# The delta rule of a two-layer model: four engines issue in the order written, steps end at each change of engine, the output gate runs ahead of the state's update, and score products move beside the state products

## Chip, cores and metric

The kernel runs on one NeuronCore of a Trainium2 chip. The core has TensorE (PE, matrix products), VectorE (DVE), ScalarE (ACT) and GpSimd (POOL), each with its own queue of instructions, and a SyncE queue (SP) that issues DMAs. TensorE writes its products to eight PSUM banks. The metric is the device time of one execution in microseconds, the median over several runs.

## What is computed

Two layers on 2 sequences of 1024 tokens, width 256, all float32. The first adds a gated delta rule and a mixture of low-rank experts to its input; the second adds gated linear attention and a sparse feed-forward. The change touches the delta rule alone:

```python
qkvz = hidden_states @ W_qkvz                      # 16 key heads, 32 value heads of 128
y = silu(causal_conv(concat(q, k, v), conv_w))     # 4 taps per channel
beta, g = sigmoid(b), -exp(A_log) * softplus(a + dt_bias)
q, k = l2norm(q) * DK**-0.5, l2norm(k)             # each shared by two value heads
def step(S, inp):                                  # one token, S is 128x128 per head
    S = S * exp(gt)
    kv = einsum('hk,hkv->hv', kt, S)
    S = S + kt[:, :, None] * ((vt - kv) * bt)[:, None, :]
    return S, einsum('hk,hkv->hv', qt, S)
gated = core * silu(z)
gated = gated * rsqrt(mean(gated * gated) + EPS) * norm_w
out = gated @ W_out
```

## The kernel before

**Tiling.** The token-by-token rule is computed in chunks of 64 tokens; a tile of 128 partitions holds a chunk of each of the two sequences (`LO` and `HI`). Eight groups of 4 value heads (2 key heads) are worked through one after the other, each in 4 units of 4 chunks. Two neighbouring chunks make a *pair*; there are 64 pairs. The state `k.S` of a group stays in SBUF.

**Stages.** The loop at L886 runs once per pair, and in each step several pairs are under way at different stages:

- `conv_block` (L327): for four blocks per step, a projection `pj` on TensorE, two evictions on ACT (`raw`, `conv`), three taps on DVE (L363), a Silu on ACT. GpSimd carries the three edge tokens over (`raw`, `tails`).
- `gates_part` (L391): norms of q and k (`sq`, `ssr`, `ss`, `rsqrt_pool`), and the gate `z` of two chunks.
- `pair_scores` (L489) for pair p: DVE accumulates the decays `lb`, ACT takes their exponential, GpSimd multiplies by beta (L512), TensorE makes the products `kq` of keys with keys and queries (L520), and DVE multiplies both into `np` (L526). SP sends `np` through DRAM to get 8x8 blocks (`n8`), which `pair_lanes` inverts on DVE.
- `pair_inverse` (L610) for pair p-1: joins the 8x8 inverses to 64x64 ones: products `px` and `pyt` on TensorE, copies `xs` on ACT, add to `U` and transpose `L` on DVE, masks `natm` on GpSimd.
- `chunk_tokens` (L675): keys and values transposed (`pk`, `pv`), scaled into `ktok` (GpSimd) and `vtok` (ACT).
- `chunk_state` (L701) for the two chunks of pair p-2: `pks`, `pqs` read the state; DVE corrects `vtok` (L719); GpSimd decays the state in place (L724); ACT scales `qs` (L729); `pf` and its copy `f`; then `pS`, which updates the state, and `po`, the output. DVE adds `pS` to `k.S` (L754), then makes `qs + po` (L758) and multiplies by `z` (L760); ACT sums the squares (`gsq`, L765). In the first chunk of a group there is no state yet: L716 to L729 and L758 are left out, and ACT copies `pS` (L752).
- `chunk_output` (L769): GpSimd makes the reciprocal root (`ms`, `rms`) and scales `z` (L782), TensorE transposes it (`yT`, L786), ACT copies (`yTs`, L788), TensorE multiplies by `W_out` (`out`, L792), DVE adds to the residual.

**What sets the order.** Each stage is a generator that yields between pieces. `in_windows` (L817) takes the pieces of a step in the order of due times: each stage has a window of the step, spread over the count of its yields in an earlier step. That is only the order in which the program is written down. A scheduler then orders the instructions of each engine anew by readiness, with the written order as priority; two `issue_after` blocks (L507, L557) tie single DVE instructions behind a tap. An engine works through its queue in the order that comes out: an instruction that waits holds up those behind it. PSUM tiles all come from one pool of eight banks (`ps_tile`).

## Time and profile before

| | |
|---|---|
| median of 3 runs | 2951.18 us (2948.95 to 2951.32) |
| profiled execution | 2948.61 us, of which the span is 2946.9 |
| delta rule, from first to last step | about 336 to 2570 us |
| granted TensorE clock in the steady stretch | 0.98 of full speed |
| DMA in the steady stretch | 16% of the 16 engines' time |

The profile comes from one execution. A busy time counts only working instructions; the rest of an engine's time is idle, and a list of waits tells which instruction's end ended each idle stretch. Matrix products overlap, so neighbouring ones show spans that lap over each other by about 0.1 us; the distance from start to start is what a product costs. Over all engines, the longest waits in 600 to 2400 us are (engine, line, waited for: total us, times, longest):

```profile
DVE vtok L719 <- PE pks L716: 202.7, 86, 4.2
ACT gsq L765 <- DVE z L760: 196.7, 81, 4.5
POOL raw L347 <- DVE conv L363: 148.2, 31, 6.2
```

These engines are idle for a third or more of the stretch, so such waits cost nothing by themselves.

### The profile page before, as it was taken

How to read it: one execution, taken by the hardware profiler on the slowest of the kernel's cores; microseconds unless marked ns; L12 is line 12 of the kernel's file. 1: busy time of each engine (PE TensorE's matmuls, PEld its weight loads, DVE VectorE, ACT ScalarE, POOL GpSimd, SP SyncE). 2: the span in 40 equal slices, each digit the busy share in tenths (PEclk: the TensorE clock that was granted, in tenths of full speed). 3: DMA queues.
4: the chain of work that ended last, by engine and by line, in shares of the span. 5: the costliest groups of instructions: out<-in, count | busy, mean ns of one | idle time of the engine just before them, and what ended most of it. 6: DMA issues, size and time to landing. Idle time of an engine off the chain costs nothing.

```text
span 2946.9 us, 87779 instructions
## 1 busy us (share of the span) xinstructions
PE 2647.8 (90%) x36502; PEld 1680.6 (57%) x36502; DVE 1914.8 (65%) x3845; ACT 1716.6 (58%) x4121; POOL 1516.5 (51%) x2690
## 2 busy tenths in 40 slices
PE   6998689998999899989999999999989998989997
PEld 2444356665666566655655666566655665654565
DVE  7652666676677666767767666677676677645544
ACT  4432566675666666666666667666666666544321
POOL 2222456666666666666666666666665666630000
PEclk9998899999999999999999999999999999999999
DMA  3001111111111111111111111111111111110000
GB/s 77 4 1 57 37 28 35 36 43 28 35 35 43 28 35 35 44 28 43 34 38 28 42 35 35 28 42 36 36 27 35 28 37 20 29 57 3 1 15 15
DMA packets 265965, 95.22 MB, mean 32 GB/s; under 512 B 220512, under 2 KB 244192, under 8 KB 265568
## 3 DMA queue, kind: packets, MB, share of 16 engines
q1 hardware_dynamic: 261872, 86.67, 13.2%
q8 instruction: 287, 4.70, 0.7%
q10 hardware_dynamic: 3696, 2.95, 0.4%
q14 instruction: 110, 0.90, 0.1%
HBM read 53.63 MB, written 27.53 MB: 28 GB/s over the span
## 4 chain that ended last, share of the span: by engine, by line
PE 32%; DVE 22%; ACT 13%; POOL 12%; issue 7%; DMA 7%; SPq 6%; DVEq 0%; POOLq 0%; ACTq 0%
DVE conv L363 6%; PE pj L152 5%; SPq L540 3%; PE out L792 3%; ACT gsq L765 3%; DMA n<-natd 3%; DVE qs L758 2%; DMA natd<-np 2%; DVE S L754 2%; POOL S L724 2%; DVE z L760 2%; PE y L1074 2%; POOL rn L447 2%; PE pg L152 2%; SPq L530 2%
## 5 line engine op out<-in xcount | busy, mean ns | idle before, releaser
L363 DVE SCALAR_TENSOR_TENSOR conv<-raw,convw,conv 128x512 f32<-128x512 f32 x768 | 644.3, 841 | 188.6 <-ACT conv L358 184.2
L152 PE MATMUL pj<-xnT,w 128*128 128x512 f32 x1024 | 509.4, 622 | 8.5 <-DMA w<-in_W_qkvz 8.5
L792 PE MATMUL out<-wo,yTs 128*128 128x256 f32 x1024 | 284.1, 425 | 106.7 <-ACT yTs L788 106.7
L719 DVE SCALAR_TENSOR_TENSOR vtok<-pks,neG,vtok 128x128 f32<-128x128 f32 x480 | 144.8, 342 | 251.7 <-PE pks L716 247.4
L765 ACT ACTIVATE gsq<-z 128x128 f32<-128x128 f32 x512 | 157.7, 308 | 246.3 <-DVE z L760 240.9
L152 PEld LDWEIGHTS pj<-xnT,w 128*128 128x128 f32 x1024 | 188.8, 197 | 187.0 <-issue 182.1
L792 PEld LDWEIGHTS out<-wo,yTs 128*128 128x128 f32 x1024 | 200.6, 206 | 143.0 <-ACT yTs L788 113.4
L724 POOL TENSOR_TENSOR S<-S,eEnd 128x512 f32<-128x512 f32 x224 | 257.7, 1170 | 26.7 <-PE pqs L716 26.3
L152 PE MATMUL z<-wz,xnT 128*128 128x512 f32 x512 | 240.4, 593 | 0.0
L356 ACT COPY raw<-pj 128x512 f32<-128x512 f32 x256 | 147.5, 576 | 144.3 <-PE pj L152 95.5
L754 DVE TENSOR_TENSOR S<-S,pS 128x512 f32<-128x512 f32 x224 | 148.5, 684 | 123.8 <-POOL S L724 110.8
L734 PE MATMUL pf<-vtok,invT 128*128 128x128 f32 x1024 | 167.1, 289 | 31.4 <-DVE vtok L719 31.2
L347 POOL COPY raw<-tails 128x6 f32<-128x6 f32 x192 | 68.8, 359 | 239.4 <-DVE conv L363 189.7
L358 ACT ACTIVATE conv<-pj,convw 128x512 f32<-128x512 f32 x256 | 176.9, 691 | 0.0
L729 ACT ACTIVATE qs<-pqs,neG 128x128 f32<-128x128 f32 x480 | 136.3, 365 | 56.9 <-PE pqs L716 54.9
L372 ACT ACTIVATE kq<-conv 128x512 f32<-128x512 f32 x128 | 81.3, 635 | 144.3 <-DVE conv L363 141.4
L734 PEld LDWEIGHTS pf<-vtok,invT 128*128 128x128 f32 x1024 | 135.9, 190 | 50.8 <-DVE vtok L719 43.2
L782 POOL TENSOR_TENSOR z<-z,rms 128x512 f32<-128x512 f32 x128 | 145.5, 1136 | 10.1 <-POOL rms L779 0.2
L688 POOL TENSOR_TENSOR ktok<-kt,wend 128x512 f32<-128x512 f32 x120 | 145.6, 1213 | 7.5 <-ACT kt L684 7.5
L360 POOL COPY tails<-raw 128x6 f32<-128x6 f32 x192 | 60.7, 316 | 156.5 <-ACT raw L356 156.5
L743 PE MATMUL pS<-f,ktok 64*64 64x128 f32 x3840 | 132.5, 275 | 7.6 <-ACT f L736 7.5
L603 PE MATMUL px<-L,natm 32*32 32x32 f32 x8192 | 101.7, 198 | 40.8 <-DVE L L645 22.7
(323 smaller groups left out, 5885.0 us busy)
## 6 DMA issues: line engine op xcount, KB each, us to landing
lb<-grows SPq DMA_DIRECT2D x128, 128.0 KB
natd<-np SPq DMA_DIRECT2D x128, 128.0 KB
w<-in_W_qkvz SPq DMA_DIRECT2D x16, 512.0 KB
nat<-np SPq DMA_DIRECT2D x256, 32.0 KB
n<-natd SPq DMA_DIRECT2D x512, 4.0 KB
ed<-E SPq DMA_DIRECT2D x64, 128.0 KB
U<-ed SPq DMA_DIRECT2D x64, 128.0 KB
wz<-in_W_qkvz SPq DMA_DIRECT2D x16, 256.0 KB
```

The source lines that it names most:

```text
L152: k.nc.tensor.matmul(ps, lhsT_of(kt), rhs_of(kt), start=(kt == 0), stop=(kt == KT - 1))
L356: nc.scalar.copy(chunks(raw[:, :, KSIZE - 1 :]), pv)
L358: nc.scalar.activation(chunks(y), pv, AF.Copy, scale=tap(KSIZE - 1))
L363: k.anchor = nc.vector.scalar_tensor_tensor(y, shifted, tap(j), y, ALU.mult, ALU.add).ins
L688: nc.gpsimd.tensor_tensor(pair(x.k), bcast(kt, 2, 2), bcast(wend, 3, P), ALU.mult)
L719: nc.vector.scalar_tensor_tensor(x.v[:, i, :], pks[:, i, :], at(k.neG, i), x.v[:, i, :], ALU.mult, ALU.add)
L724: nc.gpsimd.tensor_tensor(k.S[:, b], k.S[:, b], bcast(k.eEnd[:, b, t, h.h0 : h.h0 + HPG], 2, P), ALU.mult)
L734: nc.tensor.matmul(pf[:, i, :], invT[:, i, :], x.v[:, i, :], start=True, stop=True)
L754: nc.vector.tensor_tensor(k.S[:, b], k.S[:, b], pS[b], ALU.add)
L765: nc.scalar.activation(sq, x.z[:, i, :], AF.Square, accum_out=x.sumsq[:, i : i + 1])
L782: nc.gpsimd.tensor_tensor(y, y, bcast(rms, 2, P), ALU.mult)
L792: nc.tensor.matmul(po[:, 0:D], yT[:, i, :], wo[:, i, :], start=(i == 0), stop=(i == HPG - 1))
```

## The change

From `prefetch` to `pair_decays` the whole loop runs under `manual_schedule` for TensorE, ACT, DVE and GpSimd: these four take their instructions in the order in which the program is written down. SP's queue stays with the scheduler. The `issue_after` blocks go. Many more yields are set, one wherever the engine changes, so that `in_windows` interleaves the stages more finely. In `chunk_state` the lines for `qs + po` and `z` move ahead of the add to `k.S`, and the sums of squares move to the head of `chunk_output`. The products `kq` leave `pair_scores`: they become `pair_products`, called at the start of the state stage of the first chunk of pair p-2 in the same step (for the first two pairs, ahead of the step). The arithmetic is the same.

```diff
@@ conv_block, chunk_gate, unit_sums
     nc.scalar.activation(chunks(y), pv, AF.Copy, scale=tap(KSIZE - 1))
+    yield
...
-        k.anchor = nc.vector.scalar_tensor_tensor(y, shifted, tap(j), y, ALU.mult, ALU.add).ins
+        nc.vector.scalar_tensor_tensor(y, shifted, tap(j), y, ALU.mult, ALU.add)
         yield
@@ rsqrt_pool
     nc.gpsimd.tensor_tensor(out, x, k.mhalf[:, 0 : x.shape[1]], ALU.pow)
+    yield
     nc.gpsimd.tensor_tensor(t, out, out, ALU.mult)
...
     nc.gpsimd.tensor_tensor(out, out, t, ALU.mult)
+    yield
@@ pair_scores
-    with k.tc.issue_after(k.anchor):
-        nc.vector.tensor_tensor_scan(flat, flat, k.floor, -200.0, ALU.add, ALU.max)
+    nc.vector.tensor_tensor_scan(flat, flat, k.floor, -200.0, ALU.add, ALU.max)
     yield
     nc.scalar.activation(flat, flat, AF.Exp)
     yield
     nc.gpsimd.tensor_tensor(lb, lb, bcast(h.nb[:, c0 : c0 + PC], 3, CT), ALU.mult)
-    yield
-
-    kq = ps_tile(k, f"kq{pr.name}").rearrange("p (x m s i) -> p x m s i", x=PC, m=KPG, s=2)
-    for x in pr.chunks:
-        for m in range(KPG):
-            for b, rows in enumerate((LO, HI)):
-                both = of_chunk(h.kq[m], x.c, b)
-                nc.tensor.matmul(kq[rows, x.at, m], both[:, 0], both, start=True, stop=True)
     yield
     pr.np = pools.np.tile([P, 2, PC, HPG, CT], F32, tag="np", name=f"np{pr.name}")
     pairs = lambda a: a.rearrange("p x (m j) i -> p (x m) j i", m=KPG)
     for s in range(2):
-        by = kq[:, :, :, s].rearrange("p x m i -> p (x m) i")
+        by = pr.kq[:, :, :, s].rearrange("p x m i -> p (x m) i")
@@
+def pair_products(k, pr):
+
+    kq = ps_tile(k, f"kq{pr.name}").rearrange("p (x m s i) -> p x m s i", x=PC, m=KPG, s=2)
+    for x in pr.chunks:
+        for m in range(KPG):
+            for b, rows in enumerate((LO, HI)):
+                both = of_chunk(pr.h.kq[m], x.c, b)
+                k.nc.tensor.matmul(kq[rows, x.at, m], both[:, 0], both, start=True, stop=True)
+    pr.kq = kq
@@ pair_inverse, the same after each group of products
         blocks32(k, px, join, L)
         if s < 4:
             join = masked(s + 1)
+        yield
         xs = new("xs", s)
         nc.scalar.copy(xs, px)
@@ chunk_state
-def chunk_state(k, pools, x):
+def chunk_state(k, pools, x, scored=None):
...
+    if scored:
+        pair_products(k, scored)
     if not x.first:
         pks, pqs = four(k, f"pks{x.name}"), four(k, f"pqs{x.name}")
...
     yield
+    no = po
+    if not x.first:
+        nc.vector.tensor_tensor(qs, qs, po, ALU.add)
+        no = qs
+    nc.vector.tensor_tensor(x.z, no, x.z, ALU.mult)
+    yield
     if not x.last:
         for b in range(NB):
             if x.first:
...
                 nc.vector.tensor_tensor(k.S[:, b], k.S[:, b], pS[b], ALU.add)
     yield
-    no = po
-    if not x.first:
-        nc.vector.tensor_tensor(qs, qs, po, ALU.add)
-        no = qs
-    nc.vector.tensor_tensor(x.z, no, x.z, ALU.mult)
-    yield
+
+
+def chunk_output(k, pools, x):
...
     x.sumsq = pools.small.tile([P, HPG], F32, tag="sumsq", name=f"sumsq{x.name}")
@@ chunk_output
-    rsqrt_pool(k, sm, rms, ms, f"ch{x.name}")
+    yield
+    yield from rsqrt_pool(k, sm, rms, ms, f"ch{x.name}")
...
         nc.tensor.transpose(pt[:, i, :], y[:, i, :], k.ident)
+    yield
     yT = pools.work.tile([P, HPG, P], F32, tag="yT", name=f"yTs{x.name}")
     nc.scalar.copy(yT, pt)
@@ delta_layer
-        for p in range(-2, NPAIR + 3):
...
+        ordered = {nc.tensor.engine, nc.scalar.engine, nc.vector.engine, nc.gpsimd.engine}
+        with tc.manual_schedule(engines=ordered):
+            for p in range(-2, NPAIR + 3):
...
+                    if p < 2:
+                        pair_products(k, pair(p))
...
-                add("state0", 0.0, 0.5, chunk_state(k, pools, one))
+                    add("state0", 0.0, 0.5, chunk_state(k, pools, one, pair(p)))
```

More of the change, by code (lines that the diff above doesn't have):

```diff
@@ L398, in gates_part @@
         yield from unit_sums(k, pools, k.units[u + 1])
-        unit_norms(k, pools, k.units[u + 1])
-        yield
+        yield from unit_norms(k, pools, k.units[u + 1])
     if 0 <= p - 1 < NPAIR:
         for x in k.pairs[p - 1].chunks:
-            chunk_gate(k, pools, x)
-            yield
+            yield from chunk_gate(k, pools, x)
 def chunk_gate(k, pools, x):
@@ L461, in unit_norms @@
     r = sm.tile(shape, F32, tag="rn", name=f"rn{h.name}")
-    rsqrt_pool(k, sm, flat(r), flat(sse), f"un{h.name}")
+    yield
+    yield from rsqrt_pool(k, sm, flat(r), flat(sse), f"un{h.name}")
     h.norm = sm.tile([P, UCHUNK, KPG], F32, tag="norm", name=f"norm{h.name}", bufs=3)
@@ L469, in unit_norms @@
     nc.gpsimd.tensor_tensor(h.q2, h.rq, h.rq, ALU.mult)
+    yield
     rk2 = sm.tile([P, UCHUNK, KPG], F32, tag="rk2", name=f"rk2{h.name}")
@@ L482, in unit_norms @@
     nc.gpsimd.tensor_tensor(h.wend, h.nb, of(k.nrev), ALU.mult)
+    yield
 def four(k, name):
@@ L513, in pair_scores @@
     yield
-    kq = ps_tile(k, f"kq{pr.name}").rearrange("p (x m s i) -> p x m s i", x=PC, m=KPG, s=2)
-    for x in pr.chunks:
-        for m in range(KPG):
-            for b, rows in enumerate((LO, HI)):
-                both = of_chunk(h.kq[m], x.c, b)
-                nc.tensor.matmul(kq[rows, x.at, m], both[:, 0], both, start=True, stop=True)
-    yield
     pr.np = pools.np.tile([P, 2, PC, HPG, CT], F32, tag="np", name=f"np{pr.name}")
@@ L555, in at @@
         return bass.AP(a.tensor, flat(a)[:, r * W + c : r * W + c + 1].offset, [list(flat(a).ap[0])] + [[i * W + j, m] for i, j, m in dims])
-    with k.tc.issue_after(k.anchor):
-        nc.vector.tensor_copy(at(X, 0, 1, (2, 2, 4)), at(n, 0, 1, (2, 2, 4)))
+    nc.vector.tensor_copy(at(X, 0, 1, (2, 2, 4)), at(n, 0, 1, (2, 2, 4)))
     two, row, col = (4, 4, 2), (1, 0, 2), (0, 1, 2)
@@ L637, in pair_inverse @@
             join = masked(s + 1)
+        yield
         xs = new("xs", s)
@@ L642, in pair_inverse @@
         blocks32(k, pyt, xs, U)
+        yield
         nc.vector.tensor_tensor(U, U, pyt, ALU.add)
@@ L660, in pair_inverse @@
             nc.tensor.matmul(px[hi, i, :], full[lo, i, B:CT], L[lo, i, :], start=True, stop=True)
+    yield
     xs = new("xs", 5)
@@ L669, in pair_inverse @@
             nc.tensor.matmul(pyt[lo, i, :], xs[hi, i, :], U[hi, i, :], start=True, stop=True)
+    yield
     for q, copy in ((0, nc.scalar.copy), (2, nc.vector.tensor_copy)):
@@ L684, in chunk_tokens @@
         nc.scalar.copy(kt, pk[:, 0:KPG, :])
+        yield
         x.k = wk.tile([P, HPG, P], F32, tag="ktok", name=f"ktok{x.name}")
@@ L734, in chunk_state @@
         nc.tensor.matmul(pf[:, i, :], invT[:, i, :], x.v[:, i, :], start=True, stop=True)
+    yield
     f = wk.tile([P, HPG, P], F32, tag="f", name=f"f{x.name}")
@@ L748, in chunk_state @@
     yield
+    no = po
[3 more added lines that the diff above has]
+    nc.vector.tensor_tensor(x.z, no, x.z, ALU.mult)
+    yield
     if not x.last:
@@ L755, in chunk_state @@
     yield
-    no = po
-    if not x.first:
-        nc.vector.tensor_tensor(qs, qs, po, ALU.add)
-        no = qs
-    nc.vector.tensor_tensor(x.z, no, x.z, ALU.mult)
-    yield
+def chunk_output(k, pools, x):
+    nc, sm, wk, h, c = k.nc, pools.small, pools.work, x.h, x.c
     x.sumsq = pools.small.tile([P, HPG], F32, tag="sumsq", name=f"sumsq{x.name}")
@@ L766, in chunk_state @@
     yield
-def chunk_output(k, pools, x):
-    nc, sm, h, c = k.nc, pools.small, x.h, x.c
     wo = group_weights(k, pools, "o", h.grp)
@@ L777, in chunk_output @@
     rms = sm.tile([P, HPG], F32, tag="rms", name=f"rms{x.name}")
-    rsqrt_pool(k, sm, rms, ms, f"ch{x.name}")
+    yield
+    yield from rsqrt_pool(k, sm, rms, ms, f"ch{x.name}")
     nc.gpsimd.tensor_tensor(pair(rms), pair(rms), bcast(h.rq[:, c, :], 2, 2), ALU.mult)
@@ L786, in chunk_output @@
         nc.tensor.transpose(pt[:, i, :], y[:, i, :], k.ident)
+    yield
     yT = pools.work.tile([P, HPG, P], F32, tag="yT", name=f"yTs{x.name}")
@@ L792, in chunk_output @@
         nc.tensor.matmul(po[:, 0:D], yT[:, i, :], wo[:, i, :], start=(i == 0), stop=(i == HPG - 1))
+    yield
     res = k.res[:, h.t0 + c, :]
@@ L884, in delta_layer @@
         pair = lambda p: k.pairs[p] if 0 <= p < NPAIR else None
-        for p in range(-2, NPAIR + 3):
-            work = []
-            add = lambda kind, lo, hi, steps, *before: work.append((kind, lo, hi, steps, before))
-            prefetch(k, pools, p)
-            if p == NPAIR - 1:
-                silu_pending(k)
-            if p == -2:
-                for q in (0, 1):
-                    pair_decays(k, pools, pair(q))
-            add("conv0", 0.0, 0.475, conv_part(k, pools, p, 0))
-            add("conv1", 0.475, 0.95, conv_part(k, pools, p, 2), "conv0")
-            add(f"gates{p % 2}", 0.65, 1.0, gates_part(k, pools, p), "output1", "conv0")
-            if pair(p):
-                add("scores", 0.0, 0.45, pair_scores(k, pools, pair(p)))
-                add("lanes", 0.65, 0.9, pair_lanes(k, pools, pair(p)), "scores")
-            if pair(p - 1):
-                add("inverse", 0.0, 1.0, pair_inverse(k, pools, pair(p - 1)))
-                add("tokens0", 0.5, 1.0, chunk_tokens(k, pools, pair(p - 1).chunks[0]), "state0")
-            if pair(p - 2):
-                one, two = pair(p - 2).chunks
-                add("tokens1", 0.0, 0.4, chunk_tokens(k, pools, two))
-                add("state0", 0.0, 0.5, chunk_state(k, pools, one))
-                add("state1", 0.5, 1.0, chunk_state(k, pools, two), "state0", "tokens1")
-                add("output0", 0.55, 1.0, chunk_output(k, pools, one), "state0")
-            if pair(p - 3):
-                add("output1", 0.05, 0.5, chunk_output(k, pools, pair(p - 3).chunks[1]))
-            in_windows(k, *work)
-            if pair(p) and pair(p + 2):
-                pair_decays(k, pools, pair(p + 2))
@@ new lines, in delta_layer @@
+        ordered = {nc.tensor.engine, nc.scalar.engine, nc.vector.engine, nc.gpsimd.engine}
+        with tc.manual_schedule(engines=ordered):
+            for p in range(-2, NPAIR + 3):
+                work = []
+                add = lambda kind, lo, hi, steps, *before: work.append((kind, lo, hi, steps, before))
+                prefetch(k, pools, p)
+                if p == NPAIR - 1:
+                    silu_pending(k)
+                if p == -2:
+                    for q in (0, 1):
+                        pair_decays(k, pools, pair(q))
+                add("conv0", 0.0, 0.475, conv_part(k, pools, p, 0))
+                add("conv1", 0.475, 0.95, conv_part(k, pools, p, 2), "conv0")
+                add(f"gates{p % 2}", 0.65, 1.0, gates_part(k, pools, p), "output1", "conv0")
+                if pair(p):
+                    if p < 2:
+                        pair_products(k, pair(p))
+                    add("scores", 0.0, 0.45, pair_scores(k, pools, pair(p)))
+                    add("lanes", 0.65, 0.9, pair_lanes(k, pools, pair(p)), "scores")
+                if pair(p - 1):
+                    add("inverse", 0.0, 1.0, pair_inverse(k, pools, pair(p - 1)))
+                    add("tokens0", 0.5, 1.0, chunk_tokens(k, pools, pair(p - 1).chunks[0]), "state0")
+                if pair(p - 2):
+                    one, two = pair(p - 2).chunks
+                    add("tokens1", 0.0, 0.4, chunk_tokens(k, pools, two))
+                    add("state0", 0.0, 0.5, chunk_state(k, pools, one, pair(p)))
+                    add("state1", 0.5, 1.0, chunk_state(k, pools, two), "state0", "tokens1")
+                    add("output0", 0.55, 1.0, chunk_output(k, pools, one), "state0")
+                if pair(p - 3):
+                    add("output1", 0.05, 0.5, chunk_output(k, pools, pair(p - 3).chunks[1]))
+                in_windows(k, *work)
+                if pair(p) and pair(p + 2):
+                    pair_decays(k, pools, pair(p + 2))
```

## The prediction

> **What bounds the kernel now.** I read the page's busy table first, then the busy time of the delta rule's steady stretch (600 to 2400 us), then TensorE's waits in it, then one step on the timeline.

> ```profile
> span 2946.9 us, 87779 instructions
> PE 2647.8 (90%) x36502; PEld 1680.6 (57%) x36502; DVE 1914.8 (65%) x3845; ACT 1716.6 (58%) x4121; POOL 1516.5 (51%) x2690
> ```
> ```profile
> 600.00:2400.00 1800.00, 1649.40 (x26774) 1083.41 (x26774) 1243.29 (x2489) 1179.94 (x2938) 1133.32 (x2041) 0.98 0.16 35
> ```
> TensorE (first busy figure) works 1649.4 of 1800 us. The score products `kq` stand 50 times in this stretch, once per pair, so a step takes 36.0 us: 33.0 busy and **3.0 idle**. The change leaves TensorE's products as they are, so only those 3.0 us can be won: at most 62 steps x 3.0 = 186 us. What ends them:

> ```profile
> PE out L792 <- ACT yTs L788: 86.8, 44, 3.4
> PE pf L734 <- DVE vtok L719: 24.9, 38, 1.5
> PE pyt L669 <- DVE xs L663: 19.5, 13, 2.5
> PE px L603 <- DVE L L645: 10.6, 13, 1.1
> PE pS L743 <- ACT f L736: 5.6, 7, 1.0
> ```
> (Total us, times, longest.) More than half is one wait: the output product waits for ScalarE's copy `yTs`. No line names GpSimd: what it makes for TensorE, the scaled `z` that `yT` transposes, is early. The timeline of GpSimd in one step (start, us) shows why:

> ```profile
> 1259.52 1.04 POOL L782 TENSOR_TENSOR z<-z,rms 128x512 f32<-128x512 f32 x1
> 1260.52 1.56 POOL L512 TENSOR_TENSOR lb<-lb,nb 128x512 f32<-128x512 f32 x1
> ...
> 1263.64 2.48 POOL L724 TENSOR_TENSOR S<-S,eEnd 128x512 f32<-128x512 f32 x2
> ```
> `z` and `lb` go first, the decay of the state `S` last. That decay must wait for the products `pks` and `pqs`, which read the old state; in this step they end near 1261.2, and GpSimd is busy with the rest until 1263.6. DVE's add to `S` comes at 1268.94 and 1270.20, the next `pks` at 1275.56: 4.7 us of slack. So what is last today is the ACT copy, and GpSimd is off the path.

> **The change, part by part.** I compared the order of instructions in both programs, engine by engine.

> *Cheap parts.* ACT's table loads stay 154, so the exponential that moves into the first half of a step costs nothing in sum (1.28 us each). `kq` moves ahead of `pks` with the same 16 records (1.03 us): nothing gained, because its reader `np` waits for `lb` as well. No DMA is added; the loads of `lb` move by one place among SP's.

> *What goes.* ACT's copy `yTs` stood behind a projection's two evictions (`raw`, `conv`, 1.06 us from start to start) and up to three `gsq` (0.45 each); now the evictions come earlier and `gsq` after it. Of the 86.8/50 = 1.7 us per step nearly all goes. `pyt <- xs` and `px <- L` (0.6 per step) go too, as long as DVE isn't held.

> *What comes: GpSimd in issue order.* In the new order, after `pks` and `pqs` of a step's first chunk, GpSimd has: two `S`, one `natm`, two `ms`, `tails`, the power, `ktok`, four small ones, `lb`, the last `rms`, a small fill, and then `z`. The first waits for `pqs`, and everything is queued behind it. The rows:

> ```profile
> L724 POOL TENSOR_TENSOR S<-S,eEnd 128x512 f32<-128x512 f32 x170 | 195.8, 1171 | 20.2 <-PE pqs L716 20.2
> L782 POOL TENSOR_TENSOR z<-z,rms 128x512 f32<-128x512 f32 x100 | 114.3, 1143 | 7.8
> L688 POOL TENSOR_TENSOR ktok<-kt,wend 128x512 f32<-128x512 f32 x92 | 110.8, 1205 | 6.8 <-ACT kt L684 6.8
> L447 POOL TENSOR_TENSOR rms<-ms,mhalf 128x4 f32<-128x4 f32 x100 | 101.9, 1019 | 8.3
> L625 POOL TENSOR_TENSOR natm<-nat,lowT 128x256 f32<-128x256 f32 x100 | 72.2, 741 | 24.0 <-PE pyt L603 12.3 <-PE px L603 11.6
> L512 POOL TENSOR_TENSOR lb<-lb,nb 128x512 f32<-128x512 f32 x50 | 63.6, 1272 | 0.0
> ```
> (Second figure after the bar: mean ns.) By the undisturbed durations of the same lines: S 2 x 1.04, natm 0.73, ms 0.40, tails 0.19, power 1.01, ktok 1.04, four small 0.80, lb 1.04, rms 0.20, z 1.04 = 8.5 us; ten gaps of 0.08 between dependent small ones, the fill and a hand-over at each end make **9.6 us**. By the means of the rows it is 11.1.

> TensorE reaches `yT` after px 0.68, pf 1.0, pv 0.55, pj 1.8, pyt 0.69, pS 0.92, po 0.98 (start to start on the timeline) = 6.6 us after `pqs`. It then waits for `z`: 3.0 us by the low end, 4.5 by the high one. I take 9.9 for the chain, **a wait of 3.3 us**.

> The same chain holds DVE: `np` stands ahead of the add to `U`, the transpose `L`, and `qs`, `z` and `S`. `lb` ends 8.3 us after `pqs`; then DVE has np 0.68, U 0.36, L 0.40, three taps 2.1, qs 0.6, z 0.65, np 0.65, S 1.3 = 6.7, and `S` is done at 15.1. TensorE, released at 9.9, goes yT and the copy 1.3, out 1.85, pj 1.9 and is at `pks` at 14.95. `px` (its `L` at 9.8) is met, `pks` loses some 0.2. "z ahead of the state" puts 1.25 us before the state's add, and so uses up the slack.

> *Second half of the step.* From the next `pqs`: S 2.1, ms 0.55, invT 0.9, power 1.1, small ones 1.4, ktok 1.05, raw 0.25, z 1.04, hand-overs 0.3 = 8.7 us; TensorE is at `yT` after pk 0.37, pyt 0.69, pf 1.0, z 1.75, px 0.63, pj 1.75, pv 0.53, pS 0.92, po 0.98 = 8.6. With `pf` 0.2 late, because DVE's `vtok` stands behind a tap that needs ACT's `conv`, I charge 0.4. The DMA round trip from `np` to DVE's `X` took 11.8 us on the timeline (1199.6 to 1211.4); it starts later now, DVE waits for it, and by my count its next reader on TensorE has 5 us left: nothing.

> *Sum.* 3.3 + 0.2 + 0.4 + 0.3 for small hand-overs = 4.2 us idle instead of 3.0: +1.2 in 54 steps, +65 us. In the 8 steps with a group's first chunk there is no decay of `S`: GpSimd has 6.6 us from `gsq`'s end, TensorE some 5, so about 2.4 idle, -0.6 each, -5. The last two steps have no scores. 2948.6 (profiled execution: span 2946.9 and 1.7 around it) + 60 = **3009**, which I call 3010; the runs' median, 2951.2, is 2.6 above that execution, which is noise here (I count 0.2%, 6 us, as no change).

> [...] DVE runs three taps beside the two `S` and `natm`.

> ```profile
> L724 POOL TENSOR_TENSOR S<-S,eEnd x170: 1033/1041/1491, 610.6 to 2355.9; 128x512 f32<-128x512 f32 x170
> ```
> Shortest and longest `S` (ns) differ by 0.46 us and the median sits at the bottom. [...] By the row it is 0.13 each on the mean. [...]

> **Rivals.**
> - *Forecast, 0.55:* GpSimd's chain takes the place of the ACT copy as TensorE's last wait; 2975 to 3045.
> - *Same chain, longer, 0.18:* contention as in the mean rows (11.1 us). [...] For it: the means lie 0.1 to 0.2 above the medians on every large row. Against: DVE stands still for most of the chain.
> - *Faster, 0.20:* the copy's wait goes and GpSimd doesn't bind. Place: `z` at `yT`; it decides if the chain is within some 0.5 us of TensorE's 6.6. Then idle falls by 1.7, or with the DVE waits by 2.3 of 3.0: 62 x 1.7 = 105 to 143, so 2806 to 2844; half of it, 2895. For it: GpSimd is busy only 63% of the stretch and ACT is eased as described. Against: thirteen instructions behind a wait that no earlier start can lift, 9.6 us at their shortest.
> - *No change, 0.07:* wait won and wait lost agree within 0.1 us per step, at a chain of 8.7. That the order doesn't change is excluded: the comparison shows `S` ahead of `z` on GpSimd.

> **Numbers.** Range: 2920 (half of the faster case's gain is left out below it) to 3095 (the longer case at its mean and most of its spread). Chances: slower 0.74, same 0.06, faster 0.20.

> **What would show it.** Right: TensorE's largest wait becomes `yT` on GpSimd's `z`, some 54 x 3.3 = 180 us; DVE's first `np` waits 5 to 6 us per step for `lb`, above 300 us; `out <- yTs` falls below 20 us; `pks` waits a little for DVE's `S`; TensorE's busy time stays near 2648. Wrong: no wait on GpSimd at `yT`, or a step below 36.0 us; then GpSimd's chain starts earlier or runs shorter than the rows say.

## The result and the profile after

| | before | after |
|---|---|---|
| median | 2951.25 us (4 runs on the same chip) | 3152.92 us (4 runs, 3150.26 to 3156.04) |
| ratio | | 1.0679, 95% interval 1.0657 to 1.0701 |
| profiled execution, of which span | 2948.61 us, 2946.9 us | 3154.59 us, 3152.9 us |
| TensorE busy / idle in the span | 2647.8 / 299.1 us | 2744.2 / 408.7 us |
| mean granted TensorE clock | 0.971 | 0.941 |

The change costs 206 us of span. TensorE is idle for 110 us more, and it is *busy* for 96 us more, with the same number of products. The forecast was 60 us of idle time and 0 of busy time. The page of after, its span and its busy table:

```profile
span 3152.9 us, 87775 instructions
PE 2744.2 (87%) x36502; PEld 1750.9 (56%) x36502; DVE 1939.8 (62%) x3845; ACT 1738.4 (55%) x4121; POOL 1471.6 (47%) x2690
```

TensorE's waits in the whole of after (engine, line, waited for: total us, times, longest):

```profile
PE yT L806 <- POOL z L802: 211.0, 73, 4.6
PE ssr L434 <- ACT sq L426: 68.2, 31, 12.1
...
PE out L813 <- ACT yTs L809: 9.2, 11, 1.8
```

Over the whole of before, the same list had `out <- yTs` at 106.7 us, `yT <- z` at 7.6 and `ssr <- sq` at 4.3. The copy's wait has gone, GpSimd's has come, and with it one on ScalarE's squares `sq` that no step of the prediction names. This last wait is longer than its row says. The eight records of `ssr` follow the four squares one by one: in the step below two start within 0.07 us of each other, and the next two 0.45 us later. A record spans 0.59 to 0.62 us there, so the records cover the time between the squares, and the profile counts it as busy. The group before, and after:

```profile
1500.52 1.06 PE L433 MATMUL ssr<-sq,ones 128*32 128x512 f32 x8
```
```profile
1528.08 2.60 PE L434 MATMUL ssr<-sq,ones 128*32 128x512 f32 x8 [2.42 <-ACT sq L426]
```

Over the whole program `ssr` is busy for 37.4 us in before and 87.2 in after.

One step shows how. GpSimd's timeline in after (start and duration in us; what ended the idle time before it in brackets):

```profile
1504.19 2.49 POOL L742 TENSOR_TENSOR S<-S,eEnd 128x512 f32<-128x512 f32 x2 [9.01 <-DVE vtok L737]
1506.63 1.17 POOL L634 TENSOR_TENSOR natm<-nat,lowT 128x256 f32<-128x256 f32 x1
1507.77 0.65 POOL L794 TENSOR_TENSOR ms<-sumsq,q 128x4 f32<-128x4 f32 x1
...
1509.89 1.04 POOL L702 TENSOR_TENSOR ktok<-kt,wend 128x512 f32<-128x512 f32 x1
...
1511.89 1.04 POOL L519 TENSOR_TENSOR lb<-lb,nb 128x512 f32<-128x512 f32 x1
...
1513.17 1.04 POOL L802 TENSOR_TENSOR z<-z,rms 128x512 f32<-128x512 f32 x1
```

GpSimd stood still for 9.01 us with the decay of `S` at the head of its queue, and then worked without a gap: from 1504.19 to the end of `z` at 1514.2 it took 10.0 us. TensorE in the same step:

```profile
1509.58 1.05 PE L766 MATMUL po<-f,np 64*64 64x128 f32 x16
1514.27 1.11 PE L806 MATMUL yT<-ident,z 128*128 128x128 f32 x4 [3.64 <-POOL z L802]
1515.31 1.08 PE L612 MATMUL px<-L,natm 32*32 32x32 f32 x64
1516.32 3.60 PE L813 MATMUL out<-wo,yTs 128*128 128x256 f32 x8
...
1535.93 0.65 PE L806 MATMUL yT<-ident,z 128*128 128x128 f32 x4
...
1538.96 1.89 PE L813 MATMUL out<-wo,yTs 128*128 128x256 f32 x8
```

Both halves of the step make a `yT` and an `out`. In the second half `yT` takes 0.65 us and the eight records of `out` 1.89. In the first half, after a wait of 3.64 us, they take 1.11 and 3.60. The busy time and the clock of two stretches of this step (columns: stretch, its length, then busy us of PE, PEld, DVE, ACT, POOL, each with its count, granted clock, DMA share, GB/s):

```profile
1514.20:1520.00 5.80, 5.73 (x77) 4.63 (x78) 5.34 (x10) 1.59 (x3) 0.19 (x3) 0.53 0.35 71
1531.00:1545.00 14.00, 14.00 (x148) 9.11 (x142) 8.56 (x17) 6.85 (x15) 11.78 (x19) 1.00 0.09 20
```

The granted clock is 0.53 after the wait and 1.00 later. So the wait is paid twice: once as idle time and once as slower products. Over the whole program I counted the groups of eight `out` records that span over 2.9 us instead of 1.9 to 2.0: 17 of 127 in before, 45 of 128 in after. The trace also records each stretch in which half the clock was granted: 34 of them with 171.8 us in before, 69 with 375.8 us in after.

### The profile page after: what moved, and what is told of

Its sections match the earlier page's. It is cut to its first block, busy times and chain, and to the rows that moved or that the text cites. A ratio compares the mean times of both kernels' runs of the same rounds, so it can differ in the third digit from the quotient of the medians.

```text
span 3152.9 us, 87775 instructions
## 1 busy us (share of the span) xinstructions
PE 2744.2 (87%) x36502; PEld 1750.9 (56%) x36502; DVE 1939.8 (62%) x3845; ACT 1738.4 (55%) x4121; POOL 1471.6 (47%) x2690
## 3 DMA queue, kind: packets, MB, share of 16 engines
q1 hardware_dynamic: 261872, 86.67, 12.3%
## 4 chain that ended last, share of the span: by engine, by line
PE 53%; POOL 22%; ACT 10%; DVE 9%; issue 5%; DMA 1%; SPq 0%; POOLq 0%; ACTq 0%; DVEq 0%
PE pj L152 9%; PE out L813 9%; PE z L152 6%; POOL S L742 6%; DVE conv L364 3%; PE ssr L434 3%; POOL rms L450 3%; PE yT L806 2%; POOL z L802 2%; POOL ktok L702 2%; DVE vtok L737 2%; ACT raw L356 2%; ACT gsq L789 2%; ACT conv L358 2%; PE y L1101 2%
## 5 line engine op out<-in xcount | busy, mean ns | idle before, releaser
L364 DVE SCALAR_TENSOR_TENSOR conv<-raw,convw,conv 128x512 f32<-128x512 f32 x768 | 701.9, 914 | 197.9 <-ACT conv L358 186.9
L813 PE MATMUL out<-wo,yTs 128*128 128x256 f32 x1024 | 325.2, 473 | 9.3 <-ACT yTs L809 9.2
L806 PE MATMUL yT<-ident,z 128*128 128x128 f32 x512 | 97.4, 320 | 214.3 <-POOL z L802 211.0
L813 PEld LDWEIGHTS out<-wo,yTs 128*128 128x128 f32 x1024 | 234.4, 238 | 68.6 <-issue 14.7
L525 DVE TENSOR_TENSOR np<-lb,kq 128x512 f32<-128x512 f32 x128 | 87.4, 683 | 254.5 <-POOL lb L519 254.5
L809 ACT COPY yTs<-yT 128x512 f32<-128x512 f32 x128 | 75.3, 588 | 264.1 <-PE yT L806 264.1
L806 PEld LDWEIGHTS yT<-ident,z 128*128 128x128 f32 x512 | 61.9, 157 | 240.5 <-POOL z L802 230.1
L414 ACT ACTIVATE z<-z 128x512 f32<-128x512 f32 x128 | 76.6, 599 | 174.6 <-PE z L152 173.1
L450 POOL TENSOR_TENSOR rms<-ms,mhalf 128x4 f32<-128x4 f32 x128 | 145.8, 1139 | 7.2
L434 PE MATMUL ssr<-sq,ones 128*32 128x512 f32 x256 | 87.2, 665 | 68.2 <-ACT sq L426 68.2
```

Of the source, the lines that this page charges most:

```text
L364: nc.vector.scalar_tensor_tensor(y, shifted, tap(j), y, ALU.mult, ALU.add)
L434: nc.tensor.matmul(ps[r, :], k.ones[:, r], sq, start=True, stop=True)
L450: nc.gpsimd.tensor_tensor(out, x, k.mhalf[:, 0 : x.shape[1]], ALU.pow)
L806: nc.tensor.transpose(pt[:, i, :], y[:, i, :], k.ident)
L813: nc.tensor.matmul(po[:, 0:D], yT[:, i, :], wo[:, i, :], start=(i == 0), stop=(i == HPG - 1))
```

## The experiments

**Theory (A in the expectations):** the long wait at `yT` comes from where the decay of `S` stands on GpSimd, it drops TensorE's clock, and both together are the loss. **Rivals**, whose letters each expectation explains: the many yields and the in-order TensorE, ACT and DVE are what costs; the move of `kq` or of `z` costs; the squares are a loss of their own. Each experiment is the changed kernel with the edit shown, with ratios to the kernel before on the same chip.

### Is the clock part of it? Products put into the wait

Three products of 128x128 by 128x512 go ahead of the `yT` of each pair's second chunk, into its PSUM bank, where `yT` overwrites them. They are extra work and add nothing to the output.

```diff
     pt = four(k, f"yT{x.name}")
+    if x.at:
+        for i in range(FILL):
+            nc.tensor.matmul(pt.rearrange("p h d -> p (h d)"), k.ident, k.xnT[:, 0, 0:512], start=True, stop=True)
```

`FILL = 3`:

> The changed kernel with three products of 128x128 by 128x512 ahead of yT for the second chunk of each pair, written into yT's own bank and overwritten by it: about 0.9 us each, 2.7 us per step, which add nothing to the result. They stand where TensorE now waits 3.6 us. Theory A (the wait itself lets the clock fall): the granted clock rises to 0.97 or more, out after such a wait takes 2.0 us instead of 3.6, and although TensorE does 64 x 2.7 = 170 us more work the kernel gets FASTER, by 54 x 2.0 us less some 25 us in the ten steps without a long wait: 3050-3090 us. Rival C (the new order, not the wait, makes the products slower, or the clock is granted by load): no gain, 3150-3190 us, clock at 0.94 or below.

Measured: 3076.45 us, ratio 1.0437 (1.0420 to 1.0455), granted clock 0.978. The timeline of one step of TensorE, with the fillers as the first `yT` line, and then the stretch after them:

```profile
1518.35 1.05 PE L767 MATMUL po<-f,np 64*64 64x128 f32 x16
1519.34 2.84 PE L808 MATMUL yT<-xnT,ident 128*128 128x512 f32 x6
1523.06 0.66 PE L810 MATMUL yT<-ident,z 128*128 128x128 f32 x4 [0.88 <-POOL z L803]
1523.64 0.81 PE L613 MATMUL px<-L,natm 32*32 32x32 f32 x64
1524.39 1.99 PE L817 MATMUL out<-wo,yTs 128*128 128x256 f32 x8
```
```profile
1523.00:1528.80 5.80, 5.74 (x86) 3.92 (x88) 5.62 (x10) 2.20 (x5) 0.18 (x3) 1.00 0.34 68
```

`z` isn't earlier: 2.84 us of fillers and 0.88 of idle time make the old wait. But the clock stays at 1.00, `yT` takes 0.66 again and `out` 1.99. On the page TensorE is busy for 2838.1 us and idle for 234.8. The fillers' own group is 181.8 us, so the useful products take 2838.1 - 181.8 = 2656.3 instead of 2744.2. The sum of the spans closes: +182 of fillers, -174 of idle time, -88 of slower products = -80, from 3152.9 to 3072.9. A kernel with 182 us more work runs faster, so **the lowered clock alone costs about 88 us**. The trace's records of the clock agree: TensorE was busy at half clock for 134 us in before and for 300 in after, and half of the difference is 83 us. The 8 us by which the useful products still exceed before (2656.3 against 2647.8) are a balance: `ssr` alone takes some 50 us more, here as in after, and other products take less.

`FILL = 1`:

> As the filled kernel, but with one product of 0.9 us ahead of yT instead of three: some 2.7 us of TensorE's wait for z stay as idle time. Theory A: the filler costs nothing in the ordinary steps. If 2.7 us of idleness still halve the clock, the time stays at 3145-3165 us and the clock at 0.94; if the clock falls only after some 3.5 us, the time is that of three fillers or a little less, 3050-3085 us, clock 0.975; in between if it depends on where the wait falls.

Measured: 3139.55 us, ratio 1.0644 (1.0609 to 1.0678), and a clock of 0.952: just below the first range, far from the second, and so the third case, "in between if it depends on where the wait falls". One step:

```profile
1509.76 0.66 PE L810 MATMUL yT<-ident,z 128*128 128x128 f32 x4 [2.58 <-POOL z L803]
1510.35 0.81 PE L613 MATMUL px<-L,natm 32*32 32x32 f32 x64
1511.09 3.34 PE L817 MATMUL out<-wo,yTs 128*128 128x256 f32 x8
```

A wait of 2.58 us is still enough: `yT` and `px` run at nearly full speed, then `out` slows to 3.34. Here 37 of the counted `out` groups are slow, and half the clock is granted for 304 us instead of 376. Where the wait falls is looked at in the last section.

### Who orders GpSimd, or in what order?

GpSimd is given back to the scheduler; TensorE, ACT and DVE stay in issue order.

```diff
-        ordered = {nc.tensor.engine, nc.scalar.engine, nc.vector.engine, nc.gpsimd.engine}
+        ordered = {nc.tensor.engine, nc.scalar.engine, nc.vector.engine}
```

> The changed kernel, but GpSimd's order is left to the scheduler; TensorE, ACT and DVE stay in the written order. Theory A (GpSimd's queue puts the decay of S ahead of lb and z, and TensorE's wait for z also halves TensorE's clock for some us): the waits of yT for z fall from 211 us to under 40, the granted clock rises from 0.94 to at least 0.965, the time falls to 2880-2970 us. Rival B (the written order of ACT and DVE costs the time, GpSimd only shows it): above 3050 us, with other waits in the place of z's.

Measured: 3168.93 us, ratio 1.0746 (1.0730 to 1.0762). Theory A's number is missed by 200 us, the time lies in rival B's range, and the reason lies in the edit. GpSimd's timeline:

```profile
1521.88 2.03 POOL L742 TENSOR_TENSOR S<-S,eEnd 128x512 f32<-128x512 f32 x2
...
1525.27 1.04 POOL L802 TENSOR_TENSOR z<-z,rms 128x512 f32<-128x512 f32 x1
...
1526.31 1.04 POOL L519 TENSOR_TENSOR lb<-lb,nb 128x512 f32<-128x512 f32 x1
```

The scheduler, fed with this written order, put the decay ahead of `z` and `lb` too. `lb` now comes even after `z`, so that TensorE has two waits, one at `yT` and one for what DVE makes behind `np`:

```profile
1526.36 0.66 PE L806 MATMUL yT<-ident,z 128*128 128x128 f32 x4 [1.57 <-POOL raw L345]
1529.03 0.74 PE L612 MATMUL px<-L,natm 32*32 32x32 f32 x64 [2.01 <-DVE L L656]
1529.70 3.68 PE L813 MATMUL out<-wo,yTs 128*128 128x256 f32 x8
```

The profile puts the first wait down to the fill `raw`, which ends at the same moment as `z` (1526.3). Neither is long, and the clock falls again: `out` takes 3.68 us. So leaving GpSimd to the scheduler is no cure by itself. This run leaves the place of the decay, the yields and the written order of the other engines (rival B) as causes; the next ones separate them.

All four engines go back to the scheduler, with yields, moves and everything else kept:

```diff
-        with tc.manual_schedule(engines=ordered):
+        if ordered:
```

> The changed kernel without manual_schedule: yields, the place of z and of kq as changed, but the scheduler orders all four engines. On GpSimd it puts z and lb ahead of the decay of S again. Theory A: no wait of yT for z above 20 us in all, clock at 0.965 or more, time within 2% of the kernel before, 2900-3000 us. Rival F (the finer steps or the moves of z and kq do the harm): above 3080 us.

Measured: 2954.18 us, ratio 1.0011 (0.9990 to 1.0033), granted clock 0.954; no wait at `yT` for `z` among the listed ones. The time is that of before, but not its make-up: the clock is lower than expected, with half of it granted for 271 us against 172 in before (only 13 slow `out` groups, so it falls at other products), and TensorE's idle time is 28 us less. GpSimd again has `z` and `lb` ahead of the decay. So under the scheduler the yields and the moves do no harm in sum: what costs is the written order, taken literally.

### The decay moved, and nothing else

The two decays go from behind `pqs` to just ahead of the add to `S`, still in issue order. (`S` of a group's last chunk needs none.)

```diff
-        if not x.last:
-            for b in range(NB):
-                nc.gpsimd.tensor_tensor(
-                    k.S[:, b], k.S[:, b], bcast(k.eEnd[:, b, t, h.h0 : h.h0 + HPG], 2, P), ALU.mult
-                )
...
+    if not (x.first or x.last):
+        for b in range(NB):
+            nc.gpsimd.tensor_tensor(
+                k.S[:, b], k.S[:, b], bcast(k.eEnd[:, b, t, h.h0 : h.h0 + HPG], 2, P), ALU.mult
+            )
     if not x.last:
```

> The changed kernel with one edit: GpSimd's decay of S is written down behind the output's product with z, just ahead of the add to S, so that GpSimd's queue has lb and z first. Theory A: z is ready 6.8 us after pqs instead of 9.6, yT waits under 0.7 us per step (under 45 us in all), the clock is at 0.965 or more, and the time is 2860-2940 us. Rival D (the state's path is just as tight: the decay now ends late and pks waits for S): pks waits more than 1 us per step, time above 3000 us.

Measured: 2931.92 us, ratio 0.9942 (0.9927 to 0.9957), granted clock 0.976. Moving the decays takes 221 us off and beats the kernel before, with the yields, the moves and the written order of all four engines in place. That rules out rival B. TensorE's waits:

```profile
PE yT L806 <- POOL z L802: 46.2, 47, 4.3
PE ssr L434 <- ACT sq L426: 40.8, 31, 12.1
PE pks L734 <- DVE S L779: 33.3, 51, 1.6
```

The wait at `yT` falls from 211.0 to 46.2 us. `pks` now waits for `S`, 0.65 us at a time: the decay's price in its new place. TensorE's idle time falls by 162 us (408.7 to 2928.1 - 2681.7 = 246.4) and its busy time by 62. The clock's share is larger than these 62: TensorE is busy at half clock for 86 us instead of 300, and half of the difference is 107, but the spans of `pks` grow from 133.9 to 160.4 us, because part of its wait counts as busy.

The 9.01 us in which GpSimd stood still in after are not what the decay cost. What `z` needs first is `ms`, and `ms` needs the squares `gsq`, which in both kernels end 0.1 to 0.2 us before `pqs` does (medians of 61 steps). From the end of `pqs`, `ms` then starts at once in e3 and 3.66 us later in after, behind two `S` and a `natm`; `z` ends at 6.86 and at 10.01 us. So some 3.1 us per step were lost.

### The two moves

`kq` goes back behind the product `lb`, where it stood before.

```diff
     nc.gpsimd.tensor_tensor(lb, lb, bcast(h.nb[:, c0 : c0 + PC], 3, CT), ALU.mult)
     yield
+    pair_products(k, pr)
+    yield
```

> The changed kernel with kq back in pair_scores, so that its 1.03 us stand between pqs and yT again instead of ahead of pks. Theory A (kq beside the state products takes 1 us of cover from the wait for z): yT's wait for z falls from 211 us by about 54 x 1.0, and the clock falls less often: 3000-3100 us. Rival G (as the prediction has it: the place of kq is worth nothing): 3145-3165 us.

Measured: 3099.38 us, ratio 1.0507 (1.0483 to 1.0532): 54 us less than after. The wait at `yT` is 169.4 us instead of 211.0, and single ones are 2.77 us instead of 3.64. In after, the 1.03 us of `kq` stood ahead of `pks`, where TensorE had no wait to fill; back behind `lb` they stand ahead of `yT` and fill some of its wait.

The state's add goes ahead of `qs + po` and the product with `z` again:

```diff
-    no = po
-    if not x.first:
-        nc.vector.tensor_tensor(qs, qs, po, ALU.add)
-        no = qs
-    nc.vector.tensor_tensor(x.z, no, x.z, ALU.mult)
-    yield
     if not x.last:
...
                 nc.vector.tensor_tensor(k.S[:, b], k.S[:, b], pS[b], ALU.add)
     yield
+    no = po
+    if not x.first:
+        nc.vector.tensor_tensor(qs, qs, po, ALU.add)
+        no = qs
+    nc.vector.tensor_tensor(x.z, no, x.z, ALU.mult)
```

> The changed kernel with the add to S ahead of qs+po and z on DVE again, as before the change. Theory A: the state isn't late (pks waits 2 us for S in all), so nothing is won: 3140-3165 us. Rival E (z ahead of the state is what costs, through the slack of S): faster by more than 20 us.

Measured: 3170.13 us, ratio 1.0751 (1.0735 to 1.0767): 17 us more than after, just outside the expected range. `z` ahead of the state is worth a little; it costs nothing, since `pks` waits for `S` only 2.0 us in all of after.

### The squares

With the decay late, the four squares of the odd step are spread, two to a step:

```diff
+    if u + 1 < NUNIT:
+        unit_squares(k, pools, k.units[u + 1], odd)
+        yield
     if odd and u + 1 < NUNIT:
-        for m in range(KPG):
-            unit_squares(k, pools, k.units[u + 1], m)
-            yield
         yield from unit_sums(k, pools, k.units[u + 1])
```

> The kernel with the late decay, and the four squares sq taken apart: two in each step's gates stage instead of four in every second step, so that ACT has two of them, not four, ahead of the sums ssr. Theory A (what is left are single waits of TensorE on an engine's queue, each worth its own length): ssr's wait for sq falls from 41 us to under 20 in all, the time by 20-40 us against the late decay alone, to 2890-2915 us. Rival (another wait takes its place, as z's or S's): no change, 2925-2940 us.

Measured: **2891.92 us, ratio 0.9802 (0.9781 to 0.9824)**, the fastest kernel of the study. TensorE's waits:

```profile
PE yT L806 <- POOL z L802: 41.9, 51, 4.3
PE pks L734 <- DVE S L779: 35.4, 53, 1.2
...
PE ssr L434 <- ACT sq L426: 11.1, 3, 7.5
```

`ssr <- sq` falls by 30 us and the time by 40. The same edit alone, in after with its early decay:

> The changed kernel with one edit: two squares (sq) in each step instead of four in the odd one; sums and norms stay in the odd step, and GpSimd keeps its order with the decay first. A (the second missing term: the four squares stand behind invT on ScalarE and TensorE waits for them at ssr): the 68 us of ssr <- sq fall below 20 us, the wait at yT stays near 200 us with its lowered clock, and the time falls by 30 to 70 us to 3085-3125. B (the ssr wait only covers a lateness that shows up elsewhere, as at yT or np): the time stays within 15 us of 3153.

Measured: 3155.74 us, ratio 1.0716 (1.0684 to 1.0748): nothing won.

```profile
PE yT L806 <- POOL z L802: 208.0, 65, 4.5
PE px L671 <- DVE L L656: 43.4, 31, 2.5
PE ssr L434 <- ACT sq L426: 38.2, 25, 7.5
```

30 us of the wait at `ssr` go, and 43 us at a `px` come (2.8 us in after). On the timeline a gate projection `z` stood ahead of that `px` in after (1569.26 us); with one more yield in the even step it slid behind it, and DVE's `L` is late. So the wait at `ssr` isn't 68 us to be had by itself while the decay is early. Why the same edit pays beside the late decay is only argued, not shown: `lb`, and with it DVE's `np` and `L`, come earlier there (DVE's wait of `np` for `lb` is 144.8 us in e3 and 254.5 in after).

Last, the fastest kernel with `kq` back behind `lb` (the edit of e8):

> The fastest kernel so far (decay late, two squares per step, 2892 us) with the score products back behind lb. In the changed kernel with the decay early this took some 53 us off, because the products again stood in the stretch in which TensorE waited for z. With the decay late that wait is mostly gone. A (their worth was cover for the wait at yT): what is left of that wait is 42 us in 51 pieces, so at most 40 us come off: 2855-2892, and likely 2875. B (their place is worth something of its own, such as PSUM banks or the distance to np): it falls by about 50 us again, below 2850. C: np is late again and the pair's inverse with it, so it is slower, above 2900.

Measured: 2900.54 us, ratio 0.9853 (0.9828 to 0.9879). That misses the likely number and lands at the edge of C: `kq` behind `lb`, worth 54 us as cover for a long wait, is worth nothing once the wait is gone, and costs about 9 us (15 by the two ratios, since the runs were on different chips).

## Why the prediction was wrong: sign and cause right, size off

The forecast was 3010 us, up to 3095 at the upper end; 3152.92 came.

- **"Engines in issue order: `z` behind the decay on GpSimd" was right**, and shown: the chain took 10.0 us (forecast 9.9), the wait was 3.64 us (3.3), and `yT <- z` rose to 211.0 us ("some 180"). With the decay moved alone (e3) it fell to 46.2.
- **The step that failed is "TensorE's busy time stays near 2648"**, in the sum: the idle time of 4.2 us per step was the only price of the wait. The products after the wait ran at about half the clock (granted 0.53, eight `out` in 3.60 us instead of 1.89). Busy time was 2744.2, and the clock's part of it about 88 us by the fillers (e2), 83 by the records of the clock. Half clock came 35 times more often than in before (69 against 34), not once in each of the 54 steps, and for 204 us more, so 5.8 us each. With the 88 us of the fillers the forecast would have been near 3100, and with the next term near 3160, against 3152.92.
- **The term for the second half of the odd step was too small.** "0.4 us" was charged for every step's second half, and the four squares on ACT weren't looked at: they stand behind `invT`, which waits for DVE, and `ssr` waited 68.2 us. 60 us forecast and 64 more at `ssr` (68.2 - 4.3) are 124, beside the 110 us by which the idle time grew: `yT` took 203 us more instead of 178, and the waits that went (`out <- yTs` 98, `pf <- vtok` 29, `pyt <- xs` and `px <- L` 38) gave more back than the forecast allowed. That the wait at `ssr` could be taken away by itself is refuted by e9.
- **"`kq` ahead of `pks`: nothing gained"** missed the other side: something was lost. Its 1.03 us had stood in the wait; e8 measures 54 us for its move in this program, idle time and clock together.
- **"`z` ahead of the state uses up the slack, `pks` loses 0.2"**: the loss didn't come (2.0 us in all). The slowed `out` gave `S` more time: with `out` at full speed (e2) the spans of `pks` grow from 133.9 to 148.2 us. Taken back (e4) it wins nothing.
- **"`out <- yTs` falls below 20 us"**: right, 106.7 to 9.2. **"`np` waits for `lb` 5 to 6 us per step, above 300"**: it was 254.5 us in 62 waits, 4.1 on average, because DVE's taps kept it busy for longer first:

```profile
1504.34 4.01 DVE L364 SCALAR_TENSOR_TENSOR conv<-raw,convw,conv 128x512 f32<-128x512 f32 x3
1512.97 0.69 DVE L525 TENSOR_TENSOR np<-lb,kq 128x512 f32<-128x512 f32 x1 [4.62 <-POOL lb L519]
```

- **The step from 9.6 to 9.9 us in the chain, and the upper end of 3095:** both hold an estimate of the author's for what DVE's taps and GpSimd cost each other, and no run shows either term by itself. In after three taps took 4.01 us beside `S` and `natm`, while a later single one takes 0.71. GpSimd's part was two `S` in 2.49 us instead of 2.08 and `natm` in 1.17 instead of 0.73, so 0.85 us of the chain. DVE lost more than GpSimd (4.01 us against 3 x 0.71, so 1.9), and DVE was about to wait anyway: its `np` waits 4.62 us for `lb` behind them.
- The rival "faster" needed a chain within some 0.5 us of TensorE's 6.6. It was 10.0, and no run with the early decay came near. The rival "same chain, longer" had the right direction, for a reason that isn't the one that acted.

## What to carry to other kernels

When you take the order from a scheduler, look for the instruction that waits longest for its input on each in-order queue, and put it behind everything that doesn't depend on it: here two decays ahead of about a dozen instructions on GpSimd made `z` 3.1 us late in each step and cost over 200 us; moving them, with the squares spread, made a kernel 2% faster than before. A wait of TensorE that comes back in every step may have to be charged twice, as idle time and as slower products behind it (here `out` took 3.44, 3.34 and 3.60 us instead of 1.89 behind waits of 2.17, 2.58 and 3.64), and a small product moved out of such a wait isn't free. A busy time that grows isn't all work or clock: a group of products that waits between its own records (`ssr`, `pks`) looks busy. Fix the longest wait first: the same edits of `kq` and of the squares gained 54 and 0 us before it was fixed, and -9 and 40 after it.

## What the runs showed of the hardware

In after the granted clock was 0.53 in the 5.8 us behind a wait of 3.64 us at `yT`. The limit isn't one length of wait. In after, a wait of 2.77 us at `yT` came seven times between 650 and 2540 us. Three of them (656.78, 1595.42 and 1912.50 us) were followed by an `out` of 3.78 us, and four (970.99, 1281.68, 2227.16 and 2537.73) by one of 1.99. In e5 even 2.17 us were followed by an `out` of 3.44.

```profile
966.64:970.06 3.42, 1.57 (x44) 1.33 (x35) 0.38 (x1) 2.34 (x4) 3.09 (x9) 1.00 0.02 5
970.06:973.47 3.41, 2.48 (x73) 2.15 (x74) 3.34 (x7) 0.96 (x2) 1.13 (x3) 1.00 0.18 29
973.47:976.88 3.41, 3.41 (x16) 1.91 (x17) 3.11 (x6) 1.39 (x3) 0.05 (x1) 1.00 0.50 125
1591.28:1594.69 3.41, 1.37 (x36) 1.13 (x28) 0.57 (x1) 2.15 (x4) 3.08 (x9) 1.00 0.02 5
1594.69:1598.11 3.42, 2.69 (x70) 2.20 (x71) 3.35 (x7) 0.96 (x2) 0.94 (x3) 0.50 0.18 29
1598.11:1601.52 3.41, 3.41 (x9) 2.65 (x8) 2.81 (x6) 0.63 (x1) 0.00 (x0) 0.50 0.50 125
```

Both waits are cut in two by the edge of a window. The first leaves TensorE busy for 1.57 us of its window, and the clock stays. The second leaves it busy for 1.37, and from the edge on half the clock is granted for two windows.

Counted over the traces of before and after, in windows at full clock from 330 us to the last `out`: after each of 68 windows in which TensorE was busy for less than 0.40 of the time the clock fell, and after none of 1127 in which it was busy for 0.65 or more; of 100 between, it fell after 16. So no wholly idle window was needed here: TensorE worked for 1.37 of 3.41 us in the one at 1591.28, and the clock fell. My estimate from these shares: 0.60 of 3.41 us is 2.05 us of idle time within one window, which always lowered the clock in these two traces, and 0.35 is 1.2 us, up to which it never did.
